# Layer 0 of a spatial CNN on Trainium2: GpSimd's queue for half of the first input and for the late columns of the right scans, and a hold on the other two queues

## The chip, the cores and the metric

The kernel runs on one core of one Trainium2 chip, in fp32 throughout. The metric is device time in microseconds (us) of one launch, the median of several runs. The profile is that of one further execution, with its own time.

## The reference, cut to what matters

The input x has the shape (32, 48, 64, 128): images, channels, rows, columns. Two layers of the same form follow one another, each with its own weights:

```
x = x + scans(group_norm(x, 16 groups))

def scans(v):                 # every conv1d: 48 -> 48 channels, 5 taps, padding 2
    D[0] = v[row 0];      D[h] = v[row h] + conv1d(D[h-1], down)         # over 64 rows
    U[63] = D[63];        U[h] = D[h-1] + conv1d(U[h+1], down)           # back up; for h = 0 the input is D[63]
    R[0] = U[column 0];   R[v] = U[column v] + conv1d(R[v-1], right)     # over 128 columns
    L[127] = R[127];      L[v] = R[column v] + conv1d(L[v+1], left)      # back
    return L
```

A step of a scan depends on the whole step before it, so the 63 + 63 + 127 + 127 steps of a layer are serial for any one image. Different images are independent up to here: the normalization, too, works within one image.

## The kernel before, in words

The 32 images are cut into four groups of eight. A layer's row scans (down and up) run on one group at a time, its column scans (right and left) on a pair of groups. `PHASES` lists the twelve phases in the order in which TensorE does them: rows of groups 0 and 1, columns of pair 0, rows of group 2, and so on. Eight row phases of 126 steps and four column phases of 254 steps make 2024 steps. In a step (`step`, L647 to L674) a state of 8 positions x 48 channels = 384 partitions is held as three tiles of 128 partitions; nine products of 128x128 weights (L658) go into three PSUM tiles, and VectorE adds bias and input to each (L667). In the row layout a partition is a channel at a column modulo 8, in the column layout a channel at a row modulo 8, so between an up scan and a right scan the data pass through DRAM: `move_rows` (L517) stores up rows to the tensor `upa`, and `load_unit` (L561) loads columns from it.

All 128 columns of a pair don't fit in SBUF at once. A column phase works in four quarters j of 32 columns. A quarter has six units (`UNITS`, L556: three tiles x two halves, one half for each group of the pair), and a unit is loaded by three or four transfers, one for each run of partitions that belongs to one row modulo 8 (`PIECES`): ten for the three units of a half, twenty and 6.3 MB for a quarter. Most of them go to 48 partitions, 384 KB each when all eight rows of a piece are taken at once.

Around the change the order is set by hand. `at(t, fn, ...)` puts a call into an agenda at a time t counted in steps; the agenda is emptied between the steps of the scans, and `in_order` (L203) fixes that each engine keeps the order of the program. Which instruction waits for which data follows from the tiles that they read and write. `dma` (L198, L199) puts a transfer on SP's queue unless another is named. A transfer that stands at the head of a queue and waits holds back all that is behind it on that engine. Transfers that SP and ACT issue share eight semaphores in turn, and each waits until the eighth before it in the program has landed.

`plan_cols` (L805) plans the loads of a column phase that begins at step t0. Where the phase follows the row phase of its own second group (`follows`, L800: only for phases 2 and 6, both in layer 0), the second half of quarter 0 can't be complete before the last up steps. Its loads are cut by rows: rows 32 to 63 at t0 - 31, rows 16 to 31 at t0 - 13, rows 8 to 15 at t0 - 6, rows 2 to 7 at t0 - 1.5, rows 0 and 1 at t0 (L812 to L816). All these, 40 in each of the two phases, are on ACT's queue, and so are the 20 loads of quarter 1 at t0 + 1.5 (L822). The loads of quarter 2 are on SP's queue from t0 + 8 (L825). SP's queue also carries the stores of the up rows. Quarter j must be there when step 32j of the right scan begins.

The first group has a start of its own (`first_group`, L936 to L1061). Its 64 rows come into SBUF as two parts of 32 rows (`parts[0]`, `parts[1]`); each part has two sides of 16 rows, side 0 on partitions 0 to 47 and side 1 on partitions 64 to 111. `take` (L970) loads one image's two sides of a part by `take_batch` (L486), two transfers of 48 partitions x 8 KB. Between these 32 loads of x, small transfers are let through on the same queue: an identity matrix through DRAM (`make_ident`, L954), the taps of the down weights (`load_weights`, L231, whose L238 clears the weight tile on GpSimd first), masks and biases. GpSimd and VectorE clear the partitions between the two sides (L968). VectorE takes the statistics of each image (L346), TensorE spreads the first eight rows into the row layout by the identity pieces (L994), GpSimd and ACT permute the others (L499), and then come the averages (L377), a chain of small products (L271, L275), the scaling (L553) and the first step.

Of the kernel before, what the change touches and what calls it, by code (L numbers as in the profile page):

```python
# [29 lines left out]
F32 = mybir.dt.float32  # L30
# [9 lines left out]
SIDES = (slice(0, C), slice(ODD, ODD + C))  # L40

GB = 8
E8 = 8
FULL = 128
# [47 lines left out]
def kernel(  # L92
# [8 lines left out]
    nc = tc.nc  # L101
# [6 lines left out]
    RUN = KQ * GB  # L108
# [3 lines left out]
    HALF = H // 2  # L112
    NGRP = B // GB
    BN = 512
# [8 lines left out]
    dram = ctx.enter_context(tc.tile_pool(name="dram", bufs=1, space=bass.MemoryType.DRAM))  # L123
# [30 lines left out]
    junk = early[:, 3 * WEIGHTS + NG * N :]  # L154

    def kept(name):
# [13 lines left out]
        dram.tile([2 * NG, FULL, UNIT], F32, tag=f"spill{i}", name=f"spill{i}")  # L170
        for i in range(4)
    ]


    HELD = (2, 1, 0)
# [17 lines left out]
    def by_col(t, e, j):  # L193


        return t.rearrange("c (i q n) -> i q c n", i=E8, q=NQ)[e, j]

    def dma(dst, src, queue=None):  # L198
        (queue or nc.sync).dma_start(dst, src)  # L199
# [21 lines left out]
    def pieces(o):  # L221
        return [(e, c0, c1, p0) for e, c0, c1, g, p0 in PIECES if g == o]
# [3 lines left out]
    def slots(k):  # L226

        return (0, 1, 2) if k % 2 == 0 else (2, 1, 0)
# [254 lines left out]
                for b in range(GB):  # L483
                    take_batch(g, b, h, s, nat)

    def take_batch(g, b, h, s, nat):  # L486
        n = nat.shape[-1] // W
        dma(nat[SIDES[s], b], x[g * GB + b, :, h : h + n].rearrange("c h w -> c (h w)"))

    def permute(nat, r0, perm, engines):  # L490

# [66 lines left out]
    def quarter(k, j):  # L558
        return slot[slots(k)[j % 3]].rearrange("p (o s n) -> p s o n", s=2, o=NG)

    def load_unit(k, j, i, a0=0, a1=NH, e0=0, e1=E8, queue=None):  # L561


        _, layer, pair = PHASES[k]
        o, half = UNITS[i]
        part = slice(a0 * LINE, a1 * LINE)
        for e, c0, c1, p0 in pieces(o):
            if not e0 <= e < e1:
                continue
            dma(  # L570
                quarter(k, j)[p0 : p0 + c1 - c0, half, o, part],
                by_col(ups[layer][2 * pair + half], e, j)[c0:c1, part],
                queue,
            )

    def spill_unit(k, i, back):
        _, layer, pair = PHASES[k]
        o, half = UNITS[i]
        here, there = quarter(k, 0)[:, half, o], spill[2 * layer + pair][i]
        if back:  # L580
            dma(here, there)
        else:
            dma(there, here)
# [153 lines left out]
    def at(t, fn, *args):  # L737
        agenda.append((t, len(agenda), fn, args))

    def spread(t, gen, every):  # L740


        def go(t):
            if next(gen, "end") != "end":
                at(t + every, go, t + every)
                agenda.sort(key=lambda a: a[:2])

        at(t, go, t)
# [51 lines left out]
    def follows(k):  # L800

        _, layer, pair = PHASES[k]
        return PHASES[k - 1] == ("rows", layer, 2 * pair + 1)

    def plan_cols(k, t0, prev):  # L805
        _, layer, pair = PHASES[k]
        n = 2 * NG
        after = prev == "cols"
        for i in range(n):
            if follows(k) and UNITS[i][1] == 1:  # L810
                other = nc.scalar
                at(t0 - 31 + i, load_unit, k, 0, i, 4, NH, 0, E8, other)  # L812
                at(t0 - 13 + i, load_unit, k, 0, i, 2, 4, 0, E8, other)
                at(t0 - 6 + i / n, load_unit, k, 0, i, 1, 2, 0, E8, other)
                at(t0 - 1.5, load_unit, k, 0, i, 0, 1, E8 // 4, E8, other)
                at(t0, load_unit, k, 0, i, 0, 1, 0, E8 // 4, other)  # L816
            else:
                early = 30 if after else 46 if k == 2 else 70
                at(t0 - early + 2 * i, load_unit, k, 0, i)
            if follows(k):  # L820

                at(t0 + 1.5, load_unit, k, 1, i, 0, NH, 0, E8, nc.scalar)  # L822
            else:
                at(t0 + (3 if after else -24 + 2 * i), load_unit, k, 1, i)
            at(t0 + (38 if after else 8) + 2 * i, load_unit, k, 2, i)  # L825
            at(t0 + 33 + 2 * i, spill_unit, k, i, False)
            at(t0 + 50 + 2 * i, load_unit, k, 3, i)
        final = k == len(PHASES) - 1
        left = t0 + W - 1
        end = left + W - 1  # L830
        for i in range(n):

            t = left + 64 + 2 * i if layer == 0 else left + 39.5 + 4.5 * i
            at(t, spill_unit, k, i, True)
        units = []
        for n_done, j in enumerate((3, 2, 1, 0)):
            every = 4.5
            if j == 0 and PHASES[k + 1 if not final else k][0] == "rows":
                every = 7
            units += [(left + 34 + 32 * n_done + every * i, j, i) for i in range(n)]  # L840
        stats = None
        if layer == 0:
            stats = ResultStatsV(f"r{2 * pair}"), ResultStatsA(f"r{2 * pair + 1}")
        tiles = [stage[:, i] for i in range(4)]
        if layer:
            tiles += spare_tiles[0 : 2 if final else 1]
        n = len(tiles)
        direct = [u for u in units if not (final and u[1] == 0)]

        for u, (t, j, i) in enumerate(direct):  # L850
            nat = tiles[u % n]
            o, half = UNITS[i]
            if u < n:
                at(left + 16, load_residual, k, j, i, nat)
            if layer == 0:
                if u >= n:
                    at(direct[u - n][0] + 3, load_residual, k, j, i, nat)
                at(t, add_residual, k, j, i, nat)
                at(t + 4, keep_result, k, j, i)
                unit = quarter(k, j)[:, half, o]  # L860
                if half == 0:
                    for b in range(GB):
                        at(t + 5 + b, stats[0].take, j, o, unit, b)
                else:
                    at(t + 1, stats[1].take, j, o, unit)
            else:

                at(t, add_residual, k, j, i, nat)
                at(t + 2.5, permute_unit, k, j, i, nat, (nc.gpsimd, nc.scalar, nc.scalar))
                if final or j not in HELD:  # L870
                    at(t + 4.5, store_result, k, j, i, nat)
                else:
                    at(t + 4.5, hold_result, j, i, nat)
                if final and j == 1:
                    at(t + 4.7, load_residual, k, 0, i, last_tiles(k)[i])

                if u >= 2 and u - 2 + n < len(direct):
                    at(t + 4.6, load_residual, k, *direct[u - 2 + n][1:], tiles[(u - 2) % n])
        if layer == 0:
            t = units[-1][0] + 14  # L880
            g = 2 * pair
            spread(t, scaling(f"r{g}", 1, g, stats[0], r_masks), 1)
            spread(t + 20, scaling(f"r{g + 1}", 1, g + 1, stats[1], r_masks), 1)
        if layer:

            at(left + 10, nc.scalar.copy, junk[:, BN - 1 :], quarter(k, 3)[:, 0, 0, RUN - 1 : RUN])
        if layer and not final:
            todo = [(j, half, e) for j in HELD for half in range(2) for e in range(E8)]
            for n, what in enumerate(todo):
                at(end + 63 + 1.9 * n, let_result, *what)  # L890
        if final:
            at(end + 4, last_results, k)

    def last_tiles(k):

        s = slot[slots(k)[2]].rearrange("p (i n) -> p i n", i=2 * NG)
        return [s[:, i] for i in range(2 * NG)]
# [16 lines left out]
    def wide_nat(i0, n):  # L914
        return arena[0:P, i0 : i0 + GB * n * W].rearrange("p (b m) -> p b m", b=GB)
# [20 lines left out]
    def first_group():  # L936
# [10 lines left out]
        spare = {k: wt[k].rearrange("p i n -> p (i n)") for k in ("down1", "right", "left")}  # L947
        to_row = [spare["right"][0:C, i * FULL : (i + 1) * FULL] for i in range(9)]
        to_row += [spare["left"][0:C, 0:FULL]]
        one = last[0:C, 0 : C + 1]  # L950
# [7 lines left out]

        rows = HALF // 2
        parts = [wide_nat(SLOT + i * 2 * HALF * N * 2, rows) for i in range(2)]  # L960
        nc.vector.memset(one, 0.0)
        nc.vector.memset(one[:, 0:1], 1.0)
        for b in range(2 * GB):
            if b == 2:
                nc.vector.memset(spare["right"], 0.0)
                nc.vector.memset(spare["left"], 0.0)
            i, b = divmod(b, GB)
            (nc.vector if b % 2 else nc.gpsimd).memset(parts[i][32:64, b], 0.0)  # L968

        def take(i, b):  # L970
            for s in range(2):
                take_batch(0, b, i * HALF + s * rows, s, parts[i])

        stats = InputStats("x0", GB)
        perms = [spare["down1"][0:P, 0 : W * GB]]
# [12 lines left out]
        def rows_by_product(h0, n):  # L988
            src = parts[0][0:C].rearrange("p b (r k e) -> p e r k b", k=NK, e=E8)
            for o in range(NG):  # L990
# [12 lines left out]
                    ps.rearrange("p (r n) -> p r n", n=N),  # L1003
                )

        take(0, 0)
        make_ident()
        for b in range(1, 3):
# [62 lines left out]
    done = 0  # L1071
# [65 lines left out]
```

## Time and profile before

| | |
|---|---|
| median of 3 runs | 4361.72 us (4361.31 to 4365.94) |
| the profiled execution | 4359.74 us, of which its span is 4358.0 |
| TensorE busy | 4146.8 us, 95% of the span |
| VectorE busy | 2164.3 us |
| ACT busy | 1336.8 us |
| GpSimd busy | 847.6 us |
| first step of the down scan begins | 101.86 us |
| idle TensorE ahead of the first right step | 20.59 us before 671.19 (phase 2), 20.50 us before 1973.28 (phase 6) |
| transfers by SP's and ACT's queues | 575.99 MB and 98.59 MB |

How to read the profile. "PE" is TensorE's matmul, "DVE" VectorE, "POOL" GpSimd, "SPq" and "ACTq" the transfers that these engines issue. In a line of the timeline the first number is the start, the second the time till the last of the merged instructions ends, both in us; then the engine, the line of the kernel, the operation, the tile written and the tile read, the count, and in brackets how long the engine had been idle before and what released it. A line of the waits gives the waiting instruction, what it waited for, the total in us, the count and the longest. In a list of transfers a line gives the queue, the count, the size of one and the median time from issue to landing. "q1" is SP's queue, "q10" ACT's. `step_00r` means the right scan of layer 0, pair 0.

### The profile page before, as it was taken

The page shows a single profiled execution, that of the slowest core. Times are in us where ns is not written, and L with a number is a line of the kernel's source. Part 1 is how long each engine was busy: PE and PEld are TensorE (multiplying, and loading weights), DVE is VectorE, ACT ScalarE, POOL GpSimd, SP SyncE. Part 2 cuts the span into 40 slices and gives each one's busy share as a digit, 9 for nine tenths or more (in the row PEclk, how much of TensorE's full clock was granted, in tenths as well). Part 3 has the DMA queues.
Part 4 walks back from the last instruction along what each step waited for, and adds up shares of the span by engine and source line. Part 5 has one row for each costly group of instructions (what it writes and reads, how often), then busy time and mean ns, then how long its engine had stood idle before and what let it go on. Part 6 is the DMA issues. An engine that isn't in the chain of part 4 may idle for free. (4 is left out here: it accounts for less than half of the span.)

```text
span 4358.0 us, 89939 instructions
## 1 busy us (share of the span) xinstructions
PE 4146.8 (95%) x36632; PEld 4118.3 (95%) x36632; DVE 2164.3 (50%) x6558; ACT 1336.8 (31%) x2654; POOL 847.6 (19%) x779
## 2 busy tenths in 40 slices
PE   4899998999999999998999999999999999999993
PEld 2899998999999999998999999999999999999993
DVE  6344443446665444444446665444444444444443
ACT  1593302435785535000006774503000002110122
POOL 4571001324322020000004310000000024420352
PEclk9999999999999999999999999999999999999996
DMA  9999789856999989579407989839188039989899
GB/s 185 173 190 161 113 153 195 211 112 217 227 186 156 161 155 157 89 125 207 71 1 236 217 174 143 130 55 167 34 138 191 1 78 240 246 238 161 159 209 180
DMA packets 2113470, 680.33 MB, mean 156 GB/s; under 512 B 2000160, under 2 KB 2053152, under 8 KB 2073120
## 3 DMA queue, kind: packets, MB, share of 16 engines
q1 hardware_dynamic: 2012800, 575.99, 69.9%
q10 hardware_dynamic: 100256, 98.59, 10.7%
q8 instruction: 288, 4.72, 0.5%
q14 instruction: 126, 1.03, 0.1%
HBM read 397.57 MB, written 295.98 MB: 159 GB/s over the span
## 5 line engine op out<-in xcount | busy, mean ns | idle before, releaser
L542 ACT ACTIVATE arena<-arena,offset,scale 128x256 f32<-128x256 f32 (+2 forms) x816 | 576.5, 799 | 400.7 <-DMA arena<-mid 198.2
L595 POOL TENSOR_TENSOR arena<-arena 128x2048 f32<-128x2048 f32 x80 | 363.0, 4552 | 1662.2 <-PE step_01l L658 505.7
L499 POOL COPY arena<-arena 112x256 f32<-112x256 f32 x458 | 270.8, 649 | 660.5 <-DMA arena<-in_x 433.9
L433 ACT ACTIVATE early<-arena 128x256 f32<-128x256 f32 x192 | 129.4, 674 | 692.7 <-DMA arena<-xin 552.6
L658 PE MATMUL step_01r<-arena,early 128*128 128x128 f32 x2286 | 258.3, 277 | 20.5 <-DMA arena<-upa 20.5
L658 PEld LDWEIGHTS step_01r<-arena,early 128*128 128x128 f32 x2286 | 258.0, 194 | 20.7 <-issue 20.7
L658 PE MATMUL step_00r<-arena,early 128*128 128x128 f32 x2286 | 257.4, 276 | 20.6 <-DMA arena<-upa 20.6
L658 PEld LDWEIGHTS step_00r<-arena,early 128*128 128x128 f32 x2286 | 257.1, 193 | 20.8 <-issue 20.7
L658 PE MATMUL step_11r<-arena,early 128*128 128x128 f32 x2286 | 258.8, 277 | 5.7 <-DVE arena L667 5.7
L364 ACT ACTIVATE early<-arena 112x512 f32<-112x512 f32 x192 | 121.1, 631 | 466.5 <-PE step_00r L658 239.5
L658 PEld LDWEIGHTS step_11r<-arena,early 128*128 128x128 f32 x2286 | 258.2, 193 | 6.3 <-DVE arena L667 6.1
L658 PE MATMUL step_00l<-arena,wleft 128*128 128x128 f32 x2286 | 256.3, 275 | 0.0
L658 PE MATMUL step_10r<-arena,early 128*128 128x128 f32 x2286 | 256.1, 275 | 0.0
L658 PEld LDWEIGHTS step_10r<-arena,early 128*128 128x128 f32 x2286 | 255.7, 192 | 0.3
L658 PEld LDWEIGHTS step_00l<-arena,wleft 128*128 128x128 f32 x2286 | 255.7, 192 | 0.0
L658 PE MATMUL step_10l<-arena,wleft 128*128 128x128 f32 x2286 | 255.5, 275 | 0.0
L658 PE MATMUL step_11l<-arena,wleft 128*128 128x128 f32 x2286 | 255.5, 275 | 0.0
L658 PE MATMUL step_01l<-arena,wleft 128*128 128x128 f32 x2286 | 255.4, 275 | 0.0
L658 PEld LDWEIGHTS step_10l<-arena,wleft 128*128 128x128 f32 x2286 | 255.4, 192 | 0.0
L658 PEld LDWEIGHTS step_11l<-arena,wleft 128*128 128x128 f32 x2286 | 255.4, 192 | 0.0
L658 PEld LDWEIGHTS step_01l<-arena,wleft 128*128 128x128 f32 x2286 | 255.3, 192 | 0.0
L620 ACT COPY arena<-arena 128x256 f32<-128x256 f32 x172 | 99.5, 656 | 418.5 <-POOL arena L595 148.9
(177 smaller groups left out, 7067.7 us busy)
## 6 DMA issues: line engine op xcount, KB each, us to landing
arena<-in_x SPq DMA_DIRECT2D x48, 768.0 KB, 12.7
xin<-arena SPq DMA_DIRECT2D x96, 384.0 KB, 5.4
arena<-xin SPq DMA_DIRECT2D x96, 384.0 KB, 8.1
mid<-arena SPq DMA_DIRECT2D x96, 384.0 KB, 7.8
arena<-mid SPq DMA_DIRECT2D x192, 192.0 KB, 4.3
upb<-arena SPq DMA_DIRECT2D x192, 192.0 KB, 3.9
arena<-upb SPq DMA_DIRECT2D x96, 384.0 KB, 11.8
arena<-xin SPq DMA_DIRECT2D x186, 192.0 KB, 4.3
```

The costliest lines, as they stand in the source:

```text
L364: nc.scalar.activation(junk[0:P], piece, AF.Identity, accum_out=self.sum[:, at[0], at[1]],)
L433: nc.scalar.activation(junk[:, 0:n], view[:, b], AF.Identity, accum_out=self.sum[:, i, j : j + 1])
L499: copy(dst[:, r, q], src[:, r0 + r, q])
L542: nc.scalar.activation(args[0], args[0], AF.Identity, bias=args[2], scale=args[1])
L595: eng.tensor_tensor(unit, unit, nat, ALU.add)
L620: copy(by_w(perm)[:, a], src[:, a])
L658: nc.tensor.matmul(part(whole(ps[o]), -s), weights[:, i, FULL * (o - NG * s - i + 1) : FULL * (o - NG * s - i + 2)], part(src(i), s), star ...
```

## The change

It has three parts.

- In `first_group` the side-1 half of x's first loads (16 transfers of 384 KB, to partitions 64 to 111) goes to GpSimd's queue: the first four ahead of all memsets, the other twelve behind GpSimd's eight memsets and ahead of its memset at L238 and all its permutations. The side-0 half stays on SP's queue.
- In `plan_cols`, for the two phases that `follows` selects, the 40 loads of the second half of quarter 0 go to GpSimd's queue in place of ACT's. The loads of quarter 1 stay on ACT's, those of quarter 2 on SP's.
- New: `hold_queues`. At t0 + 1.2, after the last loads of quarter 0 and ahead of those of quarter 1, SP gets a small transfer to a DRAM tile `pin` and ACT a small copy. Both read column 1 of the right scan's first tile, which the first right step writes, so both queues stand still until then.

The line numbers after the change are shifted by some lines. The diff:

```
+    pin = dram.tile([FULL, 1], F32, tag="pin", name="pin")
...
-    def take_batch(g, b, h, s, nat):
+    def take_batch(g, b, h, s, nat, queue=None):
         n = nat.shape[-1] // W
-        dma(nat[SIDES[s], b], x[g * GB + b, :, h : h + n].rearrange("c h w -> c (h w)"))
+        dma(nat[SIDES[s], b], x[g * GB + b, :, h : h + n].rearrange("c h w -> c (h w)"), queue)
...
+    def hold_queues(k):
+
+        done = quarter(k, 0)[:, 0, 0, RUN : RUN + 1]
+        dma(pin, done)
+        nc.scalar.copy(junk[:, BN - 1 :], done)
...
+        if follows(k):
+            at(t0 + 1.2, hold_queues, k)
         for i in range(n):
             if follows(k) and UNITS[i][1] == 1:
-                other = nc.scalar
+                other = nc.gpsimd
                 at(t0 - 31 + i, load_unit, k, 0, i, 4, NH, 0, E8, other)
                 at(t0 - 13 + i, load_unit, k, 0, i, 2, 4, 0, E8, other)
                 at(t0 - 6 + i / n, load_unit, k, 0, i, 1, 2, 0, E8, other)
...
-        nc.vector.memset(one, 0.0)
-        nc.vector.memset(one[:, 0:1], 1.0)
-        for b in range(2 * GB):
-            if b == 2:
-                nc.vector.memset(spare["right"], 0.0)
-                nc.vector.memset(spare["left"], 0.0)
-            i, b = divmod(b, GB)
-            (nc.vector if b % 2 else nc.gpsimd).memset(parts[i][32:64, b], 0.0)
-
-        def take(i, b):
-            for s in range(2):
-                take_batch(0, b, i * HALF + s * rows, s, parts[i])
+        def take(i, b, s=0):
+            take_batch(0, b, i * HALF + s * rows, s, parts[i], nc.gpsimd if s else nc.sync)
...
+        for b in range(4):
+            take(0, b, 1)
+        nc.vector.memset(one, 0.0)
+        nc.vector.memset(one[:, 0:1], 1.0)
+        for b in range(2 * GB):
+            if b == 2:
+                nc.vector.memset(spare["right"], 0.0)
+                nc.vector.memset(spare["left"], 0.0)
+            i, b = divmod(b, GB)
+            (nc.vector if b % 2 else nc.gpsimd).memset(parts[i][32:64, b], 0.0)
+        for b in range(4, 2 * GB):
+            take(*divmod(b, GB), 1)
         take(0, 0)
         make_ident()
```

## The prediction, made before the changed kernel ran

> **What bounds the kernel now.** I read the page's head first, then TensorE's waits, then the timeline and the transfers of the three places that the change touches.
>
> ```profile
> PE 4146.8 (95%) x36632; PEld 4118.3 (95%) x36632; DVE 2164.3 (50%) x6558; ACT 1336.8 (31%) x2654; POOL 847.6 (19%) x779
> ...
> PE rows L994 <- DMA arena<-in_x: 39.2, 1, 39.2
> PE step_00r L658 <- DMA arena<-upa: 20.6, 1, 20.6
> PE step_01r L658 <- DMA arena<-upa: 20.5, 1, 20.5
> ...
> PE ps_x L271 <- DVE mv_x_x L377: 13.9, 1, 13.9
> ```
>
> TensorE runs a serial scan and is busy 95% of the span. The matmul stream is not touched, so the change can only move the gaps. Two gaps of 20.6 and 20.5 us stand ahead of the first right step of layer 0, once for each pair of groups, where TensorE waits for transfers of the up scan's result. The start (the first step begins at 101.86 us) is the third place.
>
> The start, from the timeline and from the transfers of its first 75 us:
>
> ```profile
> 0.73 13.98 POOL L968 MEMSET arena<- 32x2048 f32 x8 [0.29 <-POOLq L1127]
> 2.56 0.87 SPq L199 DMA_DIRECT2D arena<-in_x  x2
> 39.20 16.71 PE L994 MATMUL rows<-arena,early 48*128 48x512 f32 x18 [39.20 <-DMA arena<-in_x]
> ...
> DMA packets 5701, 13.52 MB, mean 180 GB/s; under 512 B 2400, under 2 KB 4320, under 8 KB 4320
> ...
> arena<-in_x SPq DMA_DIRECT2D x30, 384.0 KB, 7.6
> ...
> 89.83 0.54 PE L271 MATMUL ps_x<-mv_x_x,mask_sb 112*112 112x8 f32 x2 [13.90 <-DVE mv_x_x L377]
> ```
>
> The DMA engines are 99% busy from 3 us on, at 180 GB/s. The 32 loads of the first x land 2.2 us apart (384 KB each), the last at 85.30. Its statistics end at 87.89, the averages at 89.78, and a chain of small operations (12.0 us from L271 at 89.83) leads to the first step. TensorE's own work in that time, the 40 matmuls of L994, ends at 75.97, 13.9 us before L271: that is slack.
>
> The boundary at 651 to 671 us:
>
> ```profile
> 659.86 14.99 ACTq L199 DMA_DIRECT2D arena<-upa  x14
> 660.49 2.29 SPq L199 DMA_DIRECT2D upa<-arena  x3
> 662.88 1.63 SPq L199 DMA_DIRECT2D arena<-upa  x3
> 667.49 5.47 SPq L199 DMA_DIRECT2D arena<-in_x  x2
> 671.19 3.98 PE L658 MATMUL step_00r<-arena,early 128*128 128x128 f32 x18 [20.59 <-DMA arena<-upa]
> ```
>
> The last up step ends at 651.0. The stores of rows 2 to 7 land till 658.51, those of rows 0 and 1 till 664.25. ACT issues the last two critical loads at 664.48 and 664.83, and they land at 670.69 and 671.06, 6.2 us later, where the same kind took 1.9 us at 660 to 662. SP's large loads for the third quarter (from 662.88) were ahead of them in the DMA engines. So 4.3 us of each gap is this collision, and some 2 more are SP waiting for the semaphores that SP and ACT share (9.0 us in six waits between 640 and 672, part of it harmless).
>
> **What the skill says.** "DMA: Bandwidth & Descriptors", section "Rules for kernel authors": two transfers to disjoint partition halves serialize, also from two issuing engines, since both use all 16 DMA engines. The trace of before nearly agrees. From 672 to 732 us two queues stand side by side with loads to many partition ranges:
>
> ```profile
> DMA packets 2531, 11.54 MB, mean 192 GB/s; under 512 B 550, under 2 KB 550, under 8 KB 1318
> ...
> q1 hardware_dynamic: 1529, 5.79, 52.5%
> q10 hardware_dynamic: 996, 5.67, 49.6%
> ```
>
> 192 GB/s with two queues against 180 with one. Sorted by whose packet met whose, 8 KB packets took 727 to 755 ns where both queues wrote the same half of the partitions and 636 to 695 where they wrote different ones (second boundary): a tenth, not a half. "SBUF — State Buffer", section "Door 1: The DMA port swizzle", speaks the other way: a transfer to partitions 0 to 63 reaches only half of the ports. The spill from 128 partitions agrees with that: its 1 MB stores land 2.6 us apart (781.38, 783.99, 786.62, 789.26), 400 GB/s. The same DMA page, section "Latency and other measured facts", gives a first byte after some 0.6 us for SP and ACT and 1 us for GpSimd; no run here shows a GpSimd transfer.
>
> **The change, part by part.** *Start.* 16 of the 32 first loads (partitions 64 to 111) go to GpSimd's queue, none is added: 12.6 MB at 180 GB/s stay 70 us. With the tenth above for the time both queues are full (some 40 us) the last x lands up to 4 us sooner; against that SP's first loads wait about 4 us longer for GpSimd's memsets, now behind four issues, while GpSimd's own four fill the engines. I take 0 for the last landing. The order of landing changes: SP's queue also holds the small loads (identity pieces, taps), and each of their packets now alternates with an 8 KB packet of 0.73 us from the other queue. About 16 small ones precede the eighth of SP's own first-half loads, at up to 3 packets per DMA engine: up to 16 x 2.2 = 35 us. Since GpSimd's queue stands still behind its memsets for part of that time, I take a third to a half of it, 11 to 20. L994 would then start at 50 to 60 in place of 39.2 and end (36.8 us later) at 87 to 97 against L271 at 89.83. The slack of 13.9 covers most: I take +2, from 0 to +8. The memset L238 moves from 14.78 to after twelve issues, about 33 to 38 us; the taps that wait for it are issued from 37.90, so nothing is late by it.
>
> *Critical loads to GpSimd* (40 a boundary). Let c be the time of one issue on GpSimd. No row shows it: from below it is ACT's 0.31 to 0.45, from above I take 1.3 (an estimate: the page's 1 us plus ACT's 0.3). The page's extra 0.4 us on top of 0.45 gives 0.85; I take 0.9, the range being kept. Rows 8 to 15 are stored at 647.6, so ten issues end at 647.6 + 10c. Stores of rows 2 to 7 no longer wait for semaphores held by ACT's loads: landed about 656.7 (658.51 less 1.8 of the 3.1 us of SP's longest such wait, to 650.22; the rest goes to the stores' own 0.9 us each, 1152 packets of 13 ns over 16 engines). Eight issues, then the last two (their stores land about 660, before that in all cases below), and 1.9 to land: T = max(656.7, 647.6 + 10c) + 8c + 2c + 1.9.
> - c = 0.5: 663.6, 7.6 us sooner than 671.19
> - c = 0.8: 666.6, 4.6 sooner
> - c = 0.9: 667.6, 3.6 sooner
> - c = 1.0: 669.5, 1.7 sooner
> - c = 1.3: 675.5, 4.3 later.
>
> *The hold.* SP's pin transfer and ACT's copy wait for the first right step's first VectorE write. Behind them stand ACT's 20 loads of the second quarter, SP's loads of the third and two of the next x; the 4.3 us of collision are gone (contained in the 1.9 above). What is late next: the second quarter, which step 32 needs. Before, from SP's first such load at 662.88 to the last landing of the second quarter at 732.10 were 69.2 us at 192 GB/s, and VectorE took it at 736.61, 65.4 after the right scan's start: 4.5 us of slack. After, the same transfers begin at T + 2.9, last about 67.7 (no critical loads among them) and land at T + 70.6: a new stall of 5.2 us at step 32. At the second boundary 66.9 us (1964.72 to 2031.66) and 66.3 of time give T + 68.8 or somewhat more: 3 us. The hold itself costs two tiny instructions, hidden by the scan.
>
> *Sum.* Two boundaries at c = 0.9: 2 x -3.6 = -7.2, the two stalls +8.2, the start +2: +3.0 us. The profiled execution took 4359.74 (its span 4358.0), so 4362.7; the median of the runs lies 2.0 above it, so 4364.7, said as 4365. A measurement can tell about 0.2%, 8.7 us, from no change.
>
> **The rivals.**
> - *The halves do overlap* (12%): GpSimd's loads fill the ports that SP's leave idle and the first x is complete at some 70 instead of 85. For it: 400 GB/s with 128 partitions. Against it: 192 GB/s with two queues. First step 15 us sooner, with +1 at the boundaries: 4348.
> - *GpSimd issues fast, and the second quarter is in time* (10%): c of 0.5 gives -15.2 at the boundaries, stalls of 8.2, or of about 4 if the loads run a little faster, start 0: 4350 to 4355.
> - *GpSimd's issue is the bound* (25%; slower): from c = 1.1 on, the twenty issues after row 8 is stored are the chain themselves. At c = 1.3 each boundary loses 4.3 us, +8.6, with the stalls +8.2 and start +2: 4361.7 + 18.8 = 4380.5. For it: descriptors by software; against it: no figure of this case.
> - *The start becomes bound by L994* (9%; slower): the small loads lose the alternation fully, L994 ends 8 to 15 us after L271 was due: 4371 to 4378.
> - The forecast's own case, everything within a few us: 44%, 4354 to 4370.
>
> **How the numbers follow.** Faster by over 0.2%: most of the first two rivals, 0.2. Slower: the next two, 0.34 less a little that falls within, plus the edge of the forecast's case: 0.34. Within: 0.46. The range reaches to the first rival below and past the third above: 4348 to 4383.
>
> **What would show it.** In TensorE's waits the two gaps at the first right step should be 15 to 19 us, with a new one of 2 to 7 at step 32 (some 65 us after the right scan's start) put down to arena<-upa. The DMA issues of GpSimd should be 0.8 to 1.0 us apart in the stretch before the gap's end. At the start the last in_x should land between 81 and 89 and L994 begin at 50 to 60, at 180 to 200 GB/s; a landing near 70 and over 250 GB/s is the first rival, and issues over 1.1 us apart the third. If there is no gap at step 32, the second quarter's term is wrong.

## The result, and the profile after

The changed kernel takes 4385.94 us (median of 7 runs, 4379.15 to 4393.94), the kernel before 4365.94 in as many runs (4361.31 to 4370.4): a ratio of 1.0047, 95% interval 1.0036 to 1.0059. It is slower by some 20 us, and its median lies 3 us above the upper end of the forecast range. Its profiled execution took 4390.12 us, 4.2 above its median, with a span of 4388.3.

TensorE's waits in the changed kernel (what waits, for what, total, count, longest; the lines of the kernel have moved, so L994 is L993, L658 is L665 and L667 is L674):

```profile
PE rows L993 <- DMA arena<-in_x: 60.1, 1, 60.1
PE step_01r L665 <- DMA arena<-upa: 15.3, 1, 15.3
PE step_00r L665 <- DMA arena<-upa: 14.8, 1, 14.8
...
PE step_00r L665 <- DVE arena L674: 13.9, 1, 13.9
...
PE step_01r L665 <- DVE arena L674: 6.0, 1, 6.0
```

The gaps at the first right step shrank from 20.6 and 20.5 to 14.8 and 15.3. Two new waits stand further down: 13.9 and 6.0 us at step 32 of the right scans, where VectorE itself waits for the second quarter (its line is shown below). And the products of the start begin at 60.1 and not at 39.2. The timeline shows the same in order (start, time covered, engine, line, work, idle time before it):

```profile
60.11 16.74 PE L993 MATMUL rows<-arena,early 48*128 48x512 f32 x18 [60.11 <-DMA arena<-in_x]
...
96.86 0.54 PE L272 MATMUL ps_x<-mv_x_x,mask_sb 112*112 112x8 f32 x2
...
110.72 19.49 PE L665 MATMUL step_00d<-arena,early 128*128 128x128 f32 x152 [5.42 <-DVE arena L554]
```

and at the first boundary

```profile
655.87 4.94 POOL L200 DMA_DIRECT2D arena<-upa  x10 [11.60 <-DMA upa<-arena]
664.06 3.95 POOL L200 DMA_DIRECT2D arena<-upa  x8 [3.25 <-DMA upa<-arena]
669.05 0.99 POOL L200 DMA_DIRECT2D arena<-upa  x2 [1.04 <-DMA upa<-arena]
672.33 20.05 PE L665 MATMUL step_00r<-arena,early 128*128 128x128 f32 x165 [14.80 <-DMA arena<-upa]
675.19 0.34 SPq L200 DMA_DIRECT2D pin<-arena  x1
675.55 22.68 ACTq L200 DMA_DIRECT2D arena<-upa  x8
...
694.31 5.91 PE L665 MATMUL step_00r<-arena,early 128*128 128x128 f32 x36 [1.93 <-issue]
...
756.51 0.35 DVE L674 SCALAR_TENSOR_TENSOR arena<-step_00r,bd,arena 128x128 f32<-128x128 f32 x1 [14.63 <-DMA arena<-upa]
756.92 43.31 PE L665 MATMUL step_00r<-arena,early 128*128 128x112 f32 x370 [13.93 <-DVE arena L674]
```

GpSimd issues ten transfers in 4.94 us, 0.5 us each. The hold works: after SP's last stores of up rows (at 666.2) neither SP nor ACT issues a transfer until 675.19. But then ACT needs 22.68 us to issue its first eight loads.

The two profiled executions differ by 30.3 us of span. It adds up: the start +8.9 (first step 110.72 for 101.86), the two gaps at the first right step -11.0, the new stalls +21.8 (13.93 and 5.96 at step 32, and 1.93 at 692.4, some 50 us before the first of them), all other gaps -1.8, TensorE's busy time +5.9 (4152.7 for 4146.8), and +6.6 from the last matmul to the end (81.9 for 75.3). The last can't be put down to the change: that stretch measured 71.9 to 82.7 over all the profiled executions of this study, in no clear relation to what was changed. Nor is all of the first: in the kernels whose start is that of before the first step lay between 98.7 and 107.8, mean 103.4.

### The profile page after: what moved, and what is told of

It is laid out like the page before. It is cut to its first block, busy times and chain, and to the rows that moved or that the text cites. A ratio compares the mean times of both kernels' runs of the same rounds, so it can differ in the third digit from the quotient of the medians.

```text
span 4388.3 us, 90069 instructions
## 1 busy us (share of the span) xinstructions
PE 4152.7 (95%) x36632; PEld 4123.4 (94%) x36632; DVE 2168.9 (49%) x6558; ACT 1337.4 (30%) x2656; POOL 896.5 (20%) x875
## 5 line engine op out<-in xcount | busy, mean ns | idle before, releaser
L665 PE MATMUL step_00r<-arena,early 128*128 128x128 f32 x2286 | 261.1, 278 | 30.7 <-DMA arena<-upa 14.8
L665 PEld LDWEIGHTS step_00r<-arena,early 128*128 128x128 f32 x2286 | 260.4, 195 | 31.4 <-issue 17.1
L665 PE MATMUL step_01r<-arena,early 128*128 128x128 f32 x2286 | 261.0, 278 | 21.2 <-DMA arena<-upa 15.3
L665 PEld LDWEIGHTS step_01r<-arena,early 128*128 128x128 f32 x2286 | 260.5, 195 | 21.7 <-issue 15.4
L665 PE MATMUL step_11r<-arena,early 128*128 128x128 f32 x2286 | 258.1, 276 | 3.1 <-DVE arena L674 3.1
L665 PEld LDWEIGHTS step_11r<-arena,early 128*128 128x128 f32 x2286 | 257.4, 193 | 3.7 <-DVE arena L674 3.3
L665 PE MATMUL step_00l<-arena,wleft 128*128 128x128 f32 x2286 | 256.9, 275 | 2.2 <-DVE arena L674 2.2
L665 PEld LDWEIGHTS step_00l<-arena,wleft 128*128 128x128 f32 x2286 | 255.9, 192 | 2.6 <-DVE arena L674 2.6
L665 PE MATMUL step_10r<-arena,early 128*128 128x128 f32 x2286 | 256.1, 275 | 0.0
L665 PEld LDWEIGHTS step_10r<-arena,early 128*128 128x128 f32 x2286 | 255.8, 192 | 0.3
L665 PE MATMUL step_11l<-arena,wleft 128*128 128x128 f32 x2286 | 255.5, 275 | 0.0
L665 PE MATMUL step_10l<-arena,wleft 128*128 128x128 f32 x2286 | 255.5, 275 | 0.0
L665 PE MATMUL step_01l<-arena,wleft 128*128 128x128 f32 x2286 | 255.4, 275 | 0.0
L665 PEld LDWEIGHTS step_10l<-arena,wleft 128*128 128x128 f32 x2286 | 255.4, 192 | 0.0
L665 PEld LDWEIGHTS step_11l<-arena,wleft 128*128 128x128 f32 x2286 | 255.4, 192 | 0.0
L665 PEld LDWEIGHTS step_01l<-arena,wleft 128*128 128x128 f32 x2286 | 255.3, 192 | 0.0
## 6 DMA issues: line engine op xcount, KB each, us to landing
arena<-upb SPq DMA_DIRECT2D x96, 384.0 KB, 12.1
```

The lines of the kernel that those rows point to most:

```text
L665: nc.tensor.matmul(part(whole(ps[o]), -s), weights[:, i, FULL * (o - NG * s - i + 1) : FULL * (o - NG * s - i + 2)], part(src(i), s), star ...
```

## The experiments

Theory at the outset: the start loses because SP's small transfers starve beside GpSimd's large ones; the step-32 stall is larger than forecast because of the holding transfer. Each kernel changes the kernel before unless it says otherwise. Times are medians, compared with runs of the kernel before on the same chip.

### One half of the change at a time

The start alone (`plan_cols` as before):

> Only the start of the change: half of the first x on GpSimd's queue; the boundaries as before. Theory (SP's small transfers starve beside GpSimd's large ones): L994's products begin near 60 as in the changed kernel, the first step near 110.7 in place of 101.9, both gaps at the first right step stay near 20.5, no gap at step 32; 8 to 10 us slower than before. Rival (the start's loss in the changed kernel belongs to that one execution): first step within 3 us of 101.9, time within 3 us. From the last matmul to the end: 74 us if the 81 of the changed kernel comes with its boundary part, 81 if with its start.

4375.32 for 4363.08, ratio 1.0025 (1.0014 to 1.0036). L993 began at 62.0, the first step at 113.6, both gaps at the first right step stayed (21.7, 21.1), no stall at step 32, and 78.3 us from the last matmul to the end. The loss of the start is real.

The boundaries alone (`first_group` as before):

> Only the boundaries of the change: critical loads on GpSimd, the hold on SP and ACT; the start as before. Theory: first step at 101.9; gaps at the first right step of 15 us each (5 less than before), stalls at step 32 of 14 plus 2 and of 6: 11 us slower than before, 17 if the longer end (81 us from the last matmul) goes with this part. Rival (the start is the whole loss, the boundaries even out): within 4 us of before.

4383.39 for 4363.08, ratio 1.0046 (1.0034 to 1.0058): more than the 11 to 17 expected. Gaps of 14.7 and 14.3, stalls of 12.1 (with 1.1) and 11.5, so the second boundary was worse than in the changed kernel; and TensorE's busy time was 7.5 us above that of before. From the last matmul to the end it measured 76.6, so the longer end of the changed kernel (81.9) belongs to neither half. Nor do the halves add up: alone they cost 12.2 and 20.3 us, together 20.0. Why is open.

### The holding transfer

The whole change, with a holding transfer of one row:

```
-    pin = dram.tile([FULL, 1], F32, tag="pin", name="pin")
+    pin = dram.tile([1, 1], F32, tag="pin", name="pin")
...
-        dma(pin, done)
+        dma(pin, done[0:1])
```

> The whole change, but SP's holding transfer has one partition of 4 bytes in place of 128 partitions of 4 bytes. Theory: the 128 writes of 4 bytes choke the DMA engines for 8.8 us (8 KB packets took 3.5 us beside it in place of 0.7); with one row the stall at step 32 falls by about 8.8 in phase 2 (15.9 to 7) and to nothing in phase 6 (6.0 to 0): 13 to 15 us faster than the changed kernel. Rival: the stall comes from the two loads of the next x (768 KB) that hold two of the eight shared semaphores for 24 to 30 us; then phase 2 keeps some 14 us and only phase 6 changes, at most 6 us faster.

4372.86 for 4363.08, ratio 1.0022 (1.0014 to 1.0029): 9.8 us above the kernel before, where the changed kernel is 20.0 above it. Stalls of 6.5 and 4.2. The rival, which kept 14 us in phase 2, is out; but the second boundary kept 4.2 where nothing was expected.

Then the 128 rows again, their destinations 4 KB apart (boundaries only, one execution):

```
-    pin = dram.tile([FULL, 1], F32, tag="pin", name="pin")
+    pin = dram.tile([FULL, 1024], F32, tag="pin", name="pin")
...
-        dma(pin, done)
+        dma(pin[:, 0:1], done)
```

> The boundaries of the change with the start of before, the holding transfer of 128 partitions x 4 bytes as in the change, but its 128 destinations 4 KB apart in DRAM and not side by side. If many small writes to one place are the trouble: the transfer lands in 2 to 4 us in place of 8.8, 8 KB packets beside it take 0.7 us, stalls at step 32 as with one row (6 and 4). If small writes to DRAM as such are: 8 us and more to land, packets of 3 us and more beside it, stalls of 12 to 14 and of 6 to 11.

The holding transfer of the changed kernel, from issue to landing, and this one's:

```profile
DMA to landing us min/median/max: 8.8/8.8/8.8
...
DMA to landing us min/median/max: 1.4/1.7/2.0
```

The stalls were 6.6 and 1.2, and the time of the one execution was 4364.05, that of the kernel before on this chip 4364.84. So it is 128 writes of 4 bytes side by side that block, not small writes as such. The transfers of 7.5 us within the holding transfer's time, in the changed kernel, show what it does to the others:

```profile
DMA packets 178, 0.28 MB, mean 37 GB/s; under 512 B 144, under 2 KB 144, under 8 KB 144
...
q10 hardware_dynamic: 21, 0.17, 79.7%
q1 hardware_dynamic: 157, 0.11, 35.4%
```

and 7 us from shortly after the same point with the destinations apart:

```profile
DMA packets 306, 1.07 MB, mean 152 GB/s; under 512 B 176, under 2 KB 176, under 8 KB 176
...
q10 hardware_dynamic: 86, 0.57, 48.7%
q1 hardware_dynamic: 220, 0.49, 41.2%
```

37 GB/s against 152. An 8 KB packet that began in the holding transfer's 8.8 us took 3.5 us in the median, up to 9.9, where 0.7 is usual here. The DMA engines are not idle meanwhile: by the last column the packets of the two queues fill them (79.7 and 35.4% of the 16 engines' time; packets that end after the stretch count whole), but each packet takes long.

The gap of 1.93 us at 692.4 comes from the holding transfer too, as far as the traces show. The profile gives no release for it ("issue"), and a gap of this kind stands in one other kernel only, the boundaries alone (1.07 us), which has the same holding transfer. Soon after each first right step the trace has one 16 KB packet on a queue q8, of the kind "instruction". At the first boundary it starts 19.1 us after that step in the changed kernel and 18.6 in the boundaries alone, and 11.2 to 14.2 in eleven other kernels, and TensorE goes on 1.6 us after it has landed in both. That TensorE had run out of instructions fits this; no run was made for it.

### GpSimd's queue and the hold, apart

The critical loads on GpSimd, without a hold (`other = nc.gpsimd`, nothing else):

> The start as before and no hold: only the 40 critical loads of each boundary move to GpSimd's queue. Theory (what the hold saves is the collision, what GpSimd saves is the sharing of semaphores): ACT's and SP's large loads now start even sooner and stand in front of the last critical loads, gaps of 18 to 23 us, no stall at step 32; within 4 us of before. Rival (GpSimd's queue alone gives the shorter gap): gaps of 15 and no stall, 11 us faster.

4372.23 for 4363.08, ratio 1.002 (1.001 to 1.003); gaps of 25.1 and 24.7, above the theory's range too. GpSimd's queue alone makes the gaps longer by 4 us each: ACT's loads of the second quarter no longer stand behind the critical ones in ACT's own queue, so they run ahead of them.

The hold alone, one row, the critical loads on ACT:

> The start as before, the critical loads on ACT as before, and only the hold, its transfer cut to one partition, on SP and ACT. Theory (the hold removes the 4 us of collision whoever carries the critical loads, and pays it back at step 32): gaps of 16 to 17 us at the first right step, stalls at step 32 of 6 and 4 as with the one-row hold in the whole change; with 3 us for the lower clock after the stalls 3 to 7 us slower than before. Rival (the shorter gap needs GpSimd): gaps stay at 20, 10 us and more slower.

4364.12 for 4363.01, ratio 1.0003 (0.9995 to 1.0012). Gaps of 17.3 and 16.3: the shorter gap needs the hold, not GpSimd. Stalls of 3.6 and none.

SP alone held, critical loads on GpSimd, then the same with the critical loads on ACT (in both the line with `nc.scalar.copy` is gone from `hold_queues`):

> The start as before, the critical loads on GpSimd, SP held by one row, ACT not held. Theory (ACT's 20 loads of the second quarter, no longer behind the critical ones on one queue, start while the last critical loads are still waited for): gaps of 20 to 25 us as without any hold, no stall at step 32: 0 to 9 us slower than before. Rival (SP's loads are the collision): gaps of 15, no stall, 10 us faster.

4361.81 for 4363.01, ratio 0.9996 (0.9986 to 1.0006); gaps of 20.1 and 19.7, no stall, as the theory said. With the critical loads on GpSimd the gap is thus 25 us with no queue held, 20 with SP held, and 14 to 16 with both held by a transfer that does no harm (16.3 and 13.8, 15.7 and 14.6).

> The start as before, the critical loads on ACT as before, SP alone held by one row. Theory (SP's third-quarter loads are the collision; ACT's second-quarter loads stand behind the critical ones anyway and now have the engines for themselves): gaps of 16 to 17 us, no stall at step 32, 7 to 9 us faster than before. Rival (ACT's own second-quarter loads collide as much): gaps of 19 to 21, no stall, within 3 us of before.

4362.06 for 4363.01, ratio 0.999 (0.998 to 1.0). Gaps of 17.0 and 15.7, but stalls of 3.9 and 1.4 at step 32, which were not expected: ACT, which issues a load at 682.3, issues its next at 699.9, since it waits for a shared semaphore that one of SP's loads of the next x holds (issued at 670.6, landed at 699.9).

SP's third quarter 16 steps later, with the hold on both queues by one row, first with ACT, then with GpSimd for the critical loads:

```
-            at(t0 + (38 if after else 8) + 2 * i, load_unit, k, 2, i)
+            at(t0 + (38 if after else 24 if follows(k) else 8) + 2 * i, load_unit, k, 2, i)
```

> The start as before, the critical loads on ACT as before, the hold with one row on SP and ACT, and SP's loads of the third quarter planned 16 steps later, so that the second quarter comes alone. Theory (what is left of the hold's price is the second quarter sharing the engines and the semaphores with the third): gaps of 16 to 17 us, no stall at step 32, 8 us faster than before by the gaps. Rival (the two loads of the next x alone keep the second quarter late): a stall of 3 us or more stays in phase 2, 3 to 5 us faster.

> As the run with the third quarter later, but the critical loads on GpSimd's queue. Theory (GpSimd issues one in 0.5 us and its semaphores are its own): gaps of 14 to 15 us, no stall at step 32, 11 us faster than before, 3 us faster than with ACT. Rival (GpSimd brings nothing beside the hold): the same as with ACT within 2 us.

4366.51 and 4369.04 for 4364.84, ratios 1.0006 (0.9997 to 1.0014) and 1.0007 (0.9999 to 1.0016). Gaps of 16.6 and 16.1 with ACT, 15.7 and 14.5 with GpSimd, and no stall at step 32 in either. But both have a new wait in the left scan of phase 2, at 949 and 951 us: 16.6 and 8.35 us, and neither is faster than before, where 8 and 11 us were expected. The stall wasn't removed, it moved, and not to the next quarter. In the first of the two runs:

```profile
945.40 0.22 DVE L383 TENSOR_REDUCE mean_x_x<-sum_x_x 112x8 f32<-112x64 f32 x1 [14.43 <-ACT early L365]
```

VectorE keeps the order of the program and stands at the statistics of the next group's x, for which ACT sums the images as they land. The last two loads of that x come behind the later third quarter in SP's queue. They have landed at 939.3 here, at 940.6 with GpSimd, and at 918.1 in the kernel before.

### The start

GpSimd's memsets ahead of all its loads (start only):

> Only the start of the change, with GpSimd's eight memsets ahead of all its sixteen loads, so that SP's first loads wait no longer than before. Theory (small transfers starve beside the other queue): L994 still begins at 52 to 62 us, the first step at 107 to 113. Rival (the late memsets hold SP's loads up): L994 begins at 39 to 46, the first step within 3 us of that of the kernels with the start of before (101.9 to 105.6).

4371.54 for 4363.01, ratio 1.0022 (1.0014 to 1.003). L993 began at 50.2, a little before the range, the first step at 110.9. The memsets explain some 10 us of L993's delay and nothing of the first step's.

SP's first eight loads ahead of the small transfers, then all sixteen (start only):

```
-        for b in range(1, 3):
+        for b in range(1, GB):
             take(0, b)
```

> Only the start of the change, with SP's eight loads of the first part issued one after the other and the small transfers that stood between them behind. Theory (a small transfer in SP's queue costs a turn of the other queue's 8 KB packets per packet, and so SP's loads behind it wait): the eighth load lands at 42 to 50 in place of 60 to 62, the last x at 84 to 89 in place of 91 to 94; the identity pieces are now late, so L994's line may begin as late as before, 50 to 65. Rival (GpSimd's queue gets more than half of the DMA engines whatever is in SP's): the eighth load lands at 56 or later, the last x at 91 or later.

4374.41 for 4364.84, ratio 1.0022 (1.0015 to 1.0029). The eighth load landed at 40.1, before the theory's range (60.0 in the changed kernel), and L993 began at 43.2. But the last x landed at 94.7, as the rival had it, and the first step was at 110.9. Half the theory stood and half didn't.

> Only the start of the change, with all sixteen of SP's loads of x issued ahead of the small transfers. Theory (x is late because SP's loads stand behind small ones): the DMA engines stay busy and the last x lands at 72 to 80 in place of 91 to 95; the taps, the masks and the identity pieces come after it, so L994's products begin at 45 to 70 and end at 82 to 107, and the first step is at 100 to 118 by them and not by x. Rival (two queues move the same bytes more slowly): the last x lands at 86 or later.

4375.95 for 4366.0, ratio 1.0035 (1.0021 to 1.0048). The last x landed at 65.8: not slower but 20 us sooner than before. The first step came at 113.2, by L993, which began at 65.8 after the identity pieces. The transfers from 36 to 62 us in this run,

```profile
DMA packets 1076, 6.43 MB, mean 247 GB/s; under 512 B 292, under 2 KB 292, under 8 KB 292
...
q0 software_dynamic: 539, 3.27, 51.7%
q1 hardware_dynamic: 536, 3.15, 50.1%
```

from 36 to 54 us in the changed kernel,

```profile
DMA packets 829, 3.23 MB, mean 179 GB/s; under 512 B 440, under 2 KB 440, under 8 KB 440
...
q0 software_dynamic: 395, 2.37, 77.0%
q1 hardware_dynamic: 434, 0.86, 25.8%
...
taps<-in_w SPq DMA_DIRECT2D x4, 9.0 KB, 15.0
```

and from 36 to 62 in the kernel before:

```profile
DMA packets 1851, 4.62 MB, mean 178 GB/s; under 512 B 544, under 2 KB 1397, under 8 KB 1397
...
q1 hardware_dynamic: 1850, 4.61, 101.7%
```

q0 is GpSimd's queue, q1 SP's. With large loads in both queues each gets half of the engines' time and the two halves of the partitions are written at 247 GB/s, 1.4 times one queue's 178. That it is the halves that make the difference, and not two queues full of large loads as such, was not run apart. In the changed kernel the two queues have nearly as many packets each (395 and 434), but GpSimd's are large: it has three quarters of the time, and SP's queue moves 0.86 MB, since it is full of small transfers. These land late, the taps 15.0 us after their issue in the median and 7.4 in the kernel before. The pairing of large loads takes place for a few loads only. GpSimd's sixteen loads are through at 55.8, when SP has landed six of its sixteen; it issues the rest one by one between other work. The stretches 54 to 62 and 80 to 90 us in the changed kernel (the last three columns are the granted TensorE clock, the DMA engines' busy share and GB/s):

```profile
54.00:62.00 8.00, 1.89 (x2) 0.80 (x3) 3.53 (x6) 1.93 (x3) 1.87 (x4) 1.00 0.73 124
80.00:90.00 10.00, 10.00 (x12) 3.37 (x11) 7.04 (x12) 0.58 (x1) 6.81 (x20) 1.00 0.63 117
```

Here the DMA engines are 73% and 63% busy; before they were 100% and 90% (185 and 203 GB/s). What these two stretches move less, 1.3 MB, is about as much as 180 GB/s move in 7 us, which fits the 6 us by which the last x is late (91.3 for 85.3).

The small transfers on ACT's queue (start only, `dma(*later.pop(0), nc.scalar)` in `let_go`):

> Only the start of the change, with the small transfers on ACT's queue in place of SP's. Theory: SP's loads no longer stand behind them in order, only behind the semaphores shared with ACT; the last x lands at 76 to 86, L994 begins at 40 to 58, the first step at 100 to 107, within 4 us of before in time. Rival (the shared semaphores tie SP's loads to the small transfers all the same): the last x lands at 88 or later, first step at 108 or later, 8 to 12 us slower than before.

4389.97 for 4366.0, ratio 1.0059 (1.0047 to 1.0072), the rival's outcome and worse: SP issued no load between 22.8 and 48.6 us, because its next one shares a semaphore with a small transfer on ACT's queue; the last x landed at 106, the first step was at 125.0.

Three more orders of SP's queue. Eight loads, identity pieces, then the other eight with five small transfers after each, alone and with SP's hold:

> Only the start of the change, with SP's queue in the order: eight loads of the first part, the identity pieces, then the eight loads of the second part with the masks, biases and taps between them. Theory (the order of SP's queue makes the loss): the eighth load lands near 40, L994 begins at 42 to 46 and ends at 80 to 84, the last x lands at 76 to 86, the first step at 97 to 103, 2 to 8 us faster than before. Rival (a second queue costs the start in any order): first step at 108 or later, 8 us slower or more.

> The same start, with the critical loads on ACT as before and SP alone held by one row, as in the earlier run of that. Theory: the gains add, first step at 97 to 103, gaps of 16 to 17 and stalls at step 32 of at most 4: 4 to 12 us faster than before. Rival (what the gaps give is lost again elsewhere, as in the run with the hold on SP alone, which was within 0.2%): no faster than the new start alone.

4379.58 and 4376.66 for 4365.06, ratios 1.0034 (1.0021 to 1.0048) and 1.003 (1.0017 to 1.0043). L993 began at 41.8 and ended at 81.4, but the last x landed at 90.9 and the first step came at 122.5 and 122.9. The rivals' outcomes, and the order has a part in it again: the stores of permuted rows came late, so GpSimd's copies ran at the same time as the chain of small operations ahead of the first step. A product of that chain waited 5.7 us for masks that GpSimd made after sixteen copies, and one VectorE operation of 0.17 us took 9.34 (run without the hold):

```profile
103.64 9.34 DVE L296 TENSOR_TENSOR dev_x<-dev_x 112x8 f32<-112x8 f32 x1
113.02 0.17 DVE L297 TENSOR_TENSOR dev_x<-dev_x,mv_x_x 112x8 f32<-112x8 f32 x1
```

The Trainium skill, "SBUF — State Buffer", section "Who interferes with whom", says that a VectorE instruction with two SBUF inputs and a GpSimd instruction that reads SBUF block each other. The trace agrees, and more: VectorE stood still through sixteen GpSimd copies in a row (103.7 to 113.0), not through one.

At last eight loads, identity pieces, eight loads, the first stores, masks, taps:

> Only the start of the change, SP's queue in the order: eight loads, identity pieces, eight loads, the stores of the first permuted rows, masks and biases, taps. Theory (the order of SP's queue makes the loss): L994 begins at 42 to 46 and ends at 80 to 84, the last x lands at 70 to 80 in place of 91, the masks at 85 to 95, the first step at 98 to 106, within 4 us of before. Rival (the second queue costs the start in any order): first step at 108 or later, 8 us slower or more.

4384.56 for 4365.53, ratio 1.0041 (1.0026 to 1.0056). The last x landed at 80.9, just above the theory's range, and the first step was at 101.7, within it: in this one profile the order of SP's queue alone brings the first step back to where it was before. But the time is no better, since what was put behind is missed later. TensorE's down scan in this run:

```profile
101.72 18.10 PE L665 MATMUL step_00d<-arena,early 128*128 128x128 f32 x144 [5.41 <-DVE arena L554]
131.38 18.65 PE L665 MATMUL step_00d<-arena,early 128*128 128x128 f32 x144 [11.57 <-DVE arena L674]
165.71 34.81 PE L665 MATMUL step_00d<-arena,early 128*128 128x128 f32 x288 [15.68 <-DVE arena L674]
```

Gaps of 11.6 and 15.7 in place of 10.5 (146.83) and 5.0 (187.16). The twenty loads of permuted rows that stand ahead of the longest gap are issued from 141.8 us on, in the kernel before from 123.6. This run also had the longer gaps of a start-only kernel at the boundaries (23.6, 20.8) and a mean granted clock of 0.979, against 0.982.

## Why the prediction was wrong

The forecast was +3 us on the kernel before; the changed kernel is 20 us slower than it. (4 us of the distance from 4365 to 4385.94 are not the change's: the forecast started from 4361.72, and the kernel before took 4365.94 in the seven runs of the result.) By the terms of the profile the sum was short by 13.6 us for the stalls, 5.9 for TensorE's busy time, in which the clock is, and 5.8 for the start, and too high by 3.8 for the two gaps and 1.8 for other gaps.

- **The hold (the step that failed most).** The prediction said: "The hold itself costs two tiny instructions, hidden by the scan." The holding transfer took 8.8 us and held up the loads beside it, which is what step 32 waits for. The stalls were 13.9 and 6.0, with 1.9 more ahead of the first, forecast 5.2 and 3. With one row they are 6.5 and 4.2, near the forecast, and the whole is 10 us faster. The transfer was taken as tiny because its bytes are few; what counted was its 128 adjacent destinations.
- **The second quarter's lateness** was right as a mechanism: with both queues held and the third quarter right behind it, it landed after its time at the first boundary of every run, and at the second of all but the hold alone with the loads on ACT. Its size with a harmless holding transfer, 6.5 and 4.2 or 6.6 and 1.2 beside 5.2 and 3, was right within 2 us.
- **GpSimd's time per issue** was taken at 0.9, worked out from a figure for the first byte, which is another thing; it is 0.48 to 0.52. So the rival in which it bounds the boundary never came about, and that the measured time lies near its 4380.5 is chance. The gaps fell by 5.8 and 5.2; the sum had 3.6, and its row for 0.5 said 7.6. Most of the rest is the last two issues: the sum had their stores landed by then in all cases, but in the changed kernel they wait 1.04 us for them (the line at 669.05).
- **The source of the shorter gap** was put on both GpSimd and the hold. The runs show the hold alone gives 17.3 and 16.3, GpSimd with it mostly another 1 to 2 us, and GpSimd without it makes the gap longer (25).
- **The start** was forecast at +2 (0 to 8), with L993 at 50 to 60 and the last x unmoved. Measured: +7.8 over three executions of it (110.7, 113.6, 109.2) against the mean of 103.4, L993 at 60 and the last x 6 us later. The starvation was seen, but its second consequence, that SP has most of its loads left when GpSimd's queue is empty, was not. In the changed kernel both limits meet: L993 ends at 96.9, and the averages, 4.5 us after the last x, at 95.8. L272 follows L993 without a gap (the line at 96.86), 7.0 us later than in the kernel before; that is nearly the fourth rival's picture. So an order that helps only one of the two, as those with L993 at 50.2 or the last x at 65.8, leaves the first step late.
- **Overlap of the halves** was put at a tenth, from two queues that held pieces of all partition ranges. It is 1.4 times where one queue writes only the lower and the other only the upper half. The Trainium skill, "DMA: Bandwidth & Descriptors", section "Rules for kernel authors", says they serialize; here the measurement decides against it. The forecast was saved from this error by luck: SP's queue was short of large loads.
- **The clock** was not in the sum at all. The records of the traces grant TensorE either the whole clock or half of it, and half of it in stretches of 3.4 us and multiples of that, mostly around gaps. After the stall of 13.9 us (the last three columns again clock, DMA share and GB/s):

```profile
757.00:760.50 3.50, 3.50 (x17) 3.50 (x17) 1.05 (x3) 0.00 (x0) 0.00 (x0) 0.50 1.01 190
760.50:780.00 19.50, 19.50 (x176) 19.50 (x176) 9.27 (x29) 1.45 (x4) 1.47 (x3) 1.00 0.96 241
```

At half the clock 17 matmuls take 3.5 us, at the whole clock the next 176 take 19.5. After the stall of 6.0 us it is half for 6.1 us of matmuls, after the gap of 1.93 for 3.4: 1.7 to 3.1 us lost each time. The Trainium skill, "TensorE: Matmul & The Clock Gate", section "What's actually happening", says so: after an idle window of about 3.4 us the array runs at half its clock until it has been busy for another. The traces agree with the half and with the 3.4 us, but no length of a gap decides by itself: after 3.6 us in the kernel with the hold alone the clock stayed whole, and after 3.5 us in the one with the small transfers on ACT's queue it was half for 6.8 us. Counted over the whole program, 39.8 us of the changed kernel's matmul time lie in such stretches, of the kernel before 32.3. That explains 3.7 us of the 5.9 by which TensorE's busy time rose; 2.2 stay open.

The sum with the measured terms is 7.8 - 11.0 + 21.8 - 1.8 + 5.9 = 22.7, against 20.0 between the medians. What stays open: why the two halves cost less together than one by one, and that sums of gaps and medians of the smaller effects agree only to about 5 us. The hold alone should give -3.9 by its gaps and measured +1.1 (-2 to +5). No version that beats the kernel before was found; the best, SP alone held, is at 0.999 (0.998 to 1.0).

## What to carry to other kernels

In these runs a second queue for half of a load brought more bytes per second only while both queues held large loads. A queue that mixed large loads with small ones had its small ones land late beside the other queue's large packets, and its large ones waited behind them in order. A transfer that only serves as a wait should be as small in rows as in bytes. And before holding loads back, ask which step needs them and how much slack it has: here removing a collision of 4 us used up a slack of 4.5 us, and where the third quarter was shifted too the next x came late behind it.

## What the runs showed of the hardware

- 128 writes of 4 bytes to 512 adjacent bytes of DRAM took 8.8 us, and 8 KB packets beside them took 3.5 us in the median (0.7 otherwise). The same 128 writes 4 KB apart took 1.5 and 2.0 us (one execution).
- GpSimd's queue, where nothing held it up, issued a transfer every 0.48 to 0.52 us; ACT's took 0.31 to 0.48 for one at the first boundary of the kernel before.
- Two queues with 8 KB packets, one for partitions 0 to 47, one for 64 to 111: 247 GB/s, against 178 with one queue that alternates between the two.
- A VectorE operation with two inputs in SBUF, 0.17 us by itself, stood for 9.34 us beside sixteen GpSimd copies.
- TensorE's clock was whole or half, in steps of 3.4 us. At half it did 17 matmuls in 3.5 us, at the whole clock 176 in 19.5. Half the clock followed gaps of 1.93, 3.5, 4.2, 6.0, 6.5 and 13.9 us, and didn't follow one of 3.6.
